# A differential-attention and mixture-of-experts kernel: set-up moved, statistics derived, and another order within a round

## The chip, the core and the metric

The kernel runs on one core of a Trainium2 chip. The core's engines work side by side, each on its own in-order queue: TensorE (PE, with its weight loads shown apart as PEld), VectorE (DVE), ScalarE (ACT), GpSimd (POOL) and SyncE (SP), which here only issues DMAs. They meet through semaphores. TensorE writes PSUM; VectorE and ScalarE read it[...]. The metric is the device time of one launch in microseconds; the time of a kernel is the median of its runs.

## The reference

Input x has 8 sequences of 512 tokens and 128 features, all in fp32. The first half is differential attention with 16 heads of 8 features, the second a mixture of 8 experts (hidden width 512) of which each token takes 2. Each half ends in a residual and a layer norm.

```python
s1, s2 = q @ k1.T * SCALE, q @ k2.T * SCALE          # per head, causal mask
attn = softmax(s1) - sigmoid(lambda)[head] * softmax(s2)
attn = attn / max(sum(abs(attn)), 1e-6)
x = layernorm(x + (attn @ v) @ Wo.T)                 # no scale, no shift

xn = (x - mean(x)) * rsqrt(var(x) + 1e-5) * gamma + beta
w, idx = top_k(softmax(xn @ router_w.T / 1.5), 2)
y = sum over the two experts of w * (silu(xn @ W1[e]) @ W2[e])
x = layernorm(x + y)
```

So two norms follow each other: the layer norm at the end of attention, and, on its result, the norm that feeds the router and the experts. With S1 and S2 the sums of the unnormalised exponentials E1 and E2, attn is proportional to E1 - c E2 with c = sigmoid(lambda) S1/S2, and the sum of absolute values is worked out from the sum over max(E1, c E2).

## The kernel before

**Units and slots.** Attention is tiled in units of 32 queries (Q) times 4 heads on the 128 partitions, four head groups beside each other. A sequence has 16 units (j = 0 to 15); unit j looks at L = 32 (j + 1) keys. A unit with L up to 256 has two slots, each of two head groups and both score sets; a wider one has four slots, of two groups and one set. That makes 48 slots in a sequence and 384 in all, the "score slots" of the prediction. Four units make a block of 128 tokens, and 32 blocks the input.

**A round.** `round_of(now, ahead)` (L1122) writes out by hand, for all engines, what is issued for one slot. Its order sets the order of every engine's queue:

1. TensorE: the product with V (`times_v`, tile po) for a unit whose transposed weights are complete, and after a block's last unit its first block task; then the scores of the slot ahead (`scores`, L366 and the mask L375).
2. ScalarE: the copies of transposed weights out of PSUM (`evacuate`, aT, L512), then the queue `on_act`.
3. VectorE: the negated row maxima of this slot (`maxima`, tile nm, L388 for narrow and L396 for wide units).
4. TensorE: the transposes of what was combined a round ago (`transposes`, tile pt, L487). The two weight sets are added up in PSUM by transposing both into one tile.
5. VectorE: the queue `on_dve`, which holds whatever tasks of the round before have put there.
6. VectorE and GpSimd: `combine` (L424). Ahead of a unit's first piece `ratios` forms c1 = S1 sigmoid(lambda) and c2 = c1/S2 (L418 to L422). Then VectorE computes max(c2 E2, E1) into junk and its sum (L432), and GpSimd multiplies E2 by -c2 in place (L442). It must not start before VectorE has read E2.
7. ScalarE: the exponentials of this slot with their sums (`exps`, L406); then the queue `on_dve_late` on VectorE, which finishes the silu of the experts (hT, L881).
8. One task from `misc` (blocks, projections of the next sequence), and one from `routing` if there is any; one indirect transfer on GpSimd, from `moves` (sending rows to their experts, L811) or `gathers` (fetching results, L959); and expert tasks from `experts` as far as a pace allows. At most two of these allocate PSUM tiles pm, which have two buffers.

**Blocks.** A finished block runs through `block_tasks` (L537), one task to a round: reciprocals (rd, rexp), `normalise`, `project_out` with the residual xa and its statistics, `first_norm` (x1 and its own statistics), `second_norm` (xh), `turn` (transpose to xnT), `logits`. Reciprocal square roots are a power on GpSimd (`rstd_of`, tile l_rs, L112).

**Chunks.** Blocks are routed in chunks of 6, 9, 9 and 6 blocks, with the rows sent to their experts' tiles of 128, and a last chunk of 2 that computes all experts. `route_tasks` (L639) is a list of steps of small VectorE operations; `together` joins two of them in one round (weights with chosen, starts with rows). An expert tile is `turn` (pa, xgT, ysb) and `hidden` (pz, th, hT).

**Set-up.** Ahead of the rounds come constants (memsets on GpSimd), loads, the rearranged weights wq_sb and wk_sb, sigmoid of lambda (slam, L225) and slam + 1 (L226), the copies i4 and mk for the mask (L218, L219), wo_sb (L228), the zero fill of the experts' row buffers in DRAM (L271), and the projections of the first sequence: xT (L292), q (qs, then four scaled heads qb on GpSimd, L301), k, v (vt, with eight rearranging DMAs into vr, L327).

Of the kernel before, what the change touches and what calls it, by code (L numbers as in the profile page):

```python
# [20 lines left out]
def kernel(  # L21
# [15 lines left out]
    nc = tc.nc  # L37
# [28 lines left out]
    nc.gpsimd.memset(nhalf, -0.5)  # L66
    rank = const.tile([P, CB, E], F32, name="rank")
    for e in range(E):
        nc.gpsimd.memset(rank[:, :, e : e + 1], float(E - e))
# [6 lines left out]
    nc.gpsimd.memset(before, 1.0)  # L76
    nc.gpsimd.affine_select(
        out=before,
        in_=before,
        pattern=[[1, P]],  # L80
        compare_op=ALU.is_ge,
        fill=0.0,
        base=-1,
        channel_multiplier=-1,
    )
    ones = const.tile([P, P], BF16, name="ones")
    nc.gpsimd.memset(ones, 1.0)

    upto = const.tile([P, E, E], F32, name="upto")
    for e in range(E):  # L90
        nc.gpsimd.memset(upto[:, e, : e + 1], 1.0)
        if e + 1 < E:
            nc.gpsimd.memset(upto[:, e, e + 1 :], 0.0)

    fill = const.tile([P, E, CB], F32, name="fill")
    for k in range(CB):
        nc.gpsimd.memset(fill[:, :, k : k + 1], float(P * k))
# [6 lines left out]
    for t in range(tiles_of(CB)):  # L104
        nc.gpsimd.memset(number[:, t, :], float(t))
# [28 lines left out]
    with ExitStack() as actx:  # L134
# [52 lines left out]
        for h in range(4):  # L187
            nc.scalar.dma_start(
                slam[Q * h : Q * h + Q, :],
                lam.rearrange("(g h) -> h g", h=4)[h].partition_broadcast(Q),  # L190
            )
# [5 lines left out]
        nc.scalar.dma_start(gam, gamma.unsqueeze(1))  # L197
        nc.scalar.dma_start(bet, beta.unsqueeze(1))
        nc.scalar.dma_start(rw_sb, rw)
# [14 lines left out]
        nc.vector.tensor_reduce(hm, hsel, AX.X, ALU.max)  # L214
        nc.vector.tensor_scalar_mul(hms, hm, SCALE)
        for g in range(NG):
            r = slice(32 * g, 32 * g + 32)
            nc.vector.tensor_copy(i4[r], identb[r, r].unsqueeze(1).to_broadcast([32, 4, Q]))  # L218
            nc.vector.tensor_copy(mk[r], maskb[r, r])  # L219
# [5 lines left out]
        nc.scalar.activation(slam, slam, AF.Sigmoid)  # L225
        nc.vector.tensor_scalar(slam1, slam, 1.0, None, ALU.add)  # L226
        for h in range(4):
            nc.vector.tensor_scalar_mul(wo_sb[:, h, :], won, hm[:, h : h + 1])  # L228

# [31 lines left out]
        nc.gpsimd.memset(zero, 0.0)  # L261
# [6 lines left out]

        for c in chunks:
            if c.sparse:  # L270
                nc.sync.dma_start(  # L271
                    c.xs.rearrange("(t p) d -> p t d", p=P),
                    zero.unsqueeze(1).to_broadcast([P, c.nt, D]),
                )
        chunk_of = {n: c for c in chunks for n in range(c.n0, c.n0 + c.nb)}

        def projection_tasks(b):
# [16 lines left out]
            def project_q():  # L294
                pm = ps_m.tile([P, T], F32, tag="pm", name=f"pmq_{b}")
                nc.tensor.matmul(pm, lhsT=wq_sb, rhs=xTf, start=True, stop=True)

                def spread():
                    nc.vector.tensor_copy(qs, pm)
                    for h in range(4):  # L300
                        nc.gpsimd.tensor_scalar(  # L301
                            qb[:, :, h, :],
                            qs.rearrange("p (j q) -> p j q", q=Q),
                            hms[:, h : h + 1],
                            1.0,
                            ALU.mult,
                            ALU.mult,
                        )
# [24 lines left out]
        class Unit:  # L333
# [80 lines left out]
            def ratios(self):  # L414

                sums, jj = self.blk["sums"], self.jj
                c1 = sp.tile([P, NG], F32, tag="c1", name=f"c1_{self.b}_{self.j}")
                nc.vector.tensor_mul(c1, sums[:, 0, jj, :], slam)  # L418
# [3 lines left out]
                nc.vector.tensor_mul(self.c2, c1, r2)  # L422

            def combine(self, piece):  # L424
# [5 lines left out]
                L = self.L  # L430
                for g in piece:
                    nc.vector.scalar_tensor_tensor(  # L432
                        junk[:, :L],
                        self.et[:, g, 1, :L],
                        self.c2[:, g : g + 1],
                        self.et[:, g, 0, :L],
                        ALU.mult,
                        ALU.max,
                        accum_out=self.blk["big"][:, self.jj, g : g + 1],
                    )  # L440
                for g in piece:
# [7 lines left out]
                    )  # L449
                for gs, lo, kw in self.blocks(piece):  # L450
# [86 lines left out]
        def block_tasks(b, i, blk):  # L537
# [39 lines left out]
            def project_out():  # L577
# [10 lines left out]
                def residual():  # L588
# [4 lines left out]
                    s["xa"], s["mv"], s["rs"] = xa, mv, rstd_of(bp, mv, 1, "l1")  # L593
# [3 lines left out]
            def first_norm():  # L597
                def norm():
                    x1 = s["x1"] = ch.x1[:, ci, :]
                    nc.vector.tensor_scalar(  # L600
                        x1, s["xa"], s["mv"][:, 0, 0:1], s["rs"], ALU.subtract, ALU.mult
                    )
                    mv = bp.tile([P, 1, 2], F32, tag="mv2", name=f"mv2_{n}")
                    stats_of(bp, x1, mv[:, 0, :], "l2")
                    s["mv2"], s["rs2"] = mv, rstd_of(bp, mv, 1, "l2")

                on_dve.append(norm)

            def second_norm():
                def norm():  # L610
                    if ch.sparse:
                        s["xh"] = ch.xh[:, ci, :]
                    else:
                        s["xh"] = bp.tile([P, D], F32, tag="xh", name=f"xh_{n}")
                    nc.vector.tensor_scalar(
                        s["xh"], s["x1"], s["mv2"][:, 0, 0:1], s["rs2"], ALU.subtract, ALU.mult
                    )

                on_dve.append(norm)

# [645 lines left out]
```

## Time and profile before

| | |
|---|---|
| median of 3 runs | 1222.89 us (1214.82 to 1224.34) |
| the profiled execution, its own time | 1229.11 us |
| its span | 1227.1 us |
| mean granted TensorE clock | 0.923 |
| first row maxima (L388) | 20.54 us |
| last row maxima of attention (L396) | 1105.57 us |
| indirect transfers issued on GpSimd, rows sent and rows fetched | 65.4 and 60.9 us, 60 each |

The profile belongs to one execution. "Busy" is the share of the span in which an engine has an instruction under way; TensorE's matmuls are pipelined and their ends modelled, so its busy share overstates how near it is to its peak. PEclk gives the TensorE clock that was granted, in tenths of full speed, in 40 equal slices. A line of the timeline has the start, the time, the engine, the source line, the operation, the tile written and the tile read, how many instructions are merged, and in brackets the idle time of that engine just before and what ended it. In the list of waits the engine named first stood idle until the one behind the arrow was done. Idle time of an engine that nobody waits for costs nothing.

### The profile page before, as it was taken

How to read it: one execution, taken by the hardware profiler on the slowest of the kernel's cores; microseconds unless marked ns; L12 is line 12 of the kernel's file. 1: busy time of each engine (PE TensorE's matmuls, PEld its weight loads, DVE VectorE, ACT ScalarE, POOL GpSimd, SP SyncE). 2: the span in 40 equal slices, each digit the busy share in tenths (PEclk: the TensorE clock that was granted, in tenths of full speed). 3: DMA queues.
4: the chain of work that ended last, by engine and by line, in shares of the span. 5: the costliest groups of instructions: out<-in, count | busy, mean ns of one | idle time of the engine just before them, and what ended most of it. 6: DMA issues, size and time to landing. Idle time of an engine off the chain costs nothing.

```text
span 1227.1 us, 28291 instructions
## 1 busy us (share of the span) xinstructions
PE 1101.6 (90%) x9450; PEld 779.6 (64%) x9450; DVE 948.4 (77%) x2900; ACT 782.7 (64%) x2776; POOL 543.0 (44%) x967
## 2 busy tenths in 40 slices
PE   4999899888999899989898899988899889997786
PEld 2556555555666666666566666665667667776675
DVE  4688778867888678887689888879767897975656
ACT  4578767557777667766576777776567665763221
POOL 4343434464433343356556442343643762364333
PEclk8699969878999789997899999999989998999998
DMA  8000000011121111110133113221222333435762
GB/s 245 7 8 1 10 2 8 26 59 30 30 82 45 33 42 53 46 41 23 38 99 85 57 45 91 63 56 47 72 78 72 105 107 105 126 92 149 215 188 68
DMA packets 128897, 84.30 MB, mean 69 GB/s; under 512 B 22896, under 2 KB 114288, under 8 KB 128752
## 3 DMA queue, kind: packets, MB, share of 16 engines
q1 hardware_dynamic: 110944, 68.25, 19.8%
q0 software_dynamic: 3840, 7.87, 2.3%
q10 hardware_dynamic: 13968, 6.37, 1.8%
q8 instruction: 76, 1.25, 0.4%
q14 instruction: 69, 0.57, 0.1%
HBM read 63.31 MB, written 17.56 MB: 66 GB/s over the span
## 4 chain that ended last, share of the span: by engine, by line
PE 56%; DVE 19%; ACT 10%; issue 6%; POOL 4%; DMA 4%; ACTq 0%; SPq 0%; POOLq 0%; DVEq 0%
PE pt L487 18%; PE sc L366 12%; ACT et L406 6%; PE po L529 5%; PE sc_None L366 5%; PE pa L914 5%; PE pz L934 4%; DVE junk L432 3%; DVE nm L396 3%; DVE nm L388 2%; PE pmo L580 2%; ACT aT L512 2%; DVE l_st L118 1%; DMA got<-ys,row 1%; POOL qb L301 1%
## 5 line engine op out<-in xcount | busy, mean ns | idle before, releaser
L442 POOL TENSOR_SCALAR et<-et,c 128x224 f32<-128x224 f32 (+15 forms) x512 | 266.9, 526 | 438.6 <-DVE junk L432 301.2
L487 PE MATMUL pt<-ident,et 128*128 128x128 f32 (+1 forms) x2048 | 330.0, 297 | 36.6 <-POOL et L442 20.7
L406 ACT ACTIVATE et<-sc,nm 128x512 f32<-128x512 f32 (+7 forms) x512 | 299.7, 593 | 68.8 <-DVE nm L396 46.8
L487 PEld LDWEIGHTS pt<-ident,et 128*128 128x128 f32 (+1 forms) x2048 | 231.9, 146 | 171.6 <-issue 59.9
L396 DVE TENSOR_REDUCE nm<-sc 128x2 f32<-128x576 f32 (+7 forms) x256 | 251.6, 983 | 41.8 <-PE sc L375 41.5
L432 DVE SCALAR_TENSOR_TENSOR junk<-et,c 128x224 f32<-128x224 f32 (+15 forms) x512 | 264.2, 516 | 9.6
L512 ACT COPY aT<-pt 128x384 f32<-128x384 f32 (+5 forms) x488 | 185.8, 407 | 130.5 <-PE pt L487 127.4
L366 PE MATMUL sc<-kT,qb 32*128 32x384 f32 (+7 forms) x1024 | 246.5, 558 | 13.3 <-ACT et L406 12.4
L406 ACT ACTIVATE et<-sc_None,nm 128x256 f32<-128x256 f32 (+7 forms) x512 | 188.1, 385 | 31.2 <-DVE nm L388 23.2
L366 PE MATMUL sc_None<-kT,qb 32*128 32x512 f32 (+7 forms) x512 | 118.6, 546 | 22.3 <-ACT et L406 21.1
L388 DVE TENSOR_REDUCE nm<-sc_None 128x4 f32<-128x256 f32 (+7 forms) x128 | 96.0, 751 | 40.8 <-PE sc_None L375 40.5
L366 PEld LDWEIGHTS sc<-kT,qb 32*128 32x128 f32 x1024 | 78.4, 187 | 63.7 <-ACT et L406 30.6
L112 POOL TENSOR_TENSOR l_rs<-l_ve,nhalf 128x1 f32<-128x1 f32 x96 | 62.5, 651 | 124.9 <-DVE l_ve L110 102.8
L934 PE MATMUL pz<-xgT,w 128*128 128x128 f32 x704 | 101.5, 291 | 11.4 <-DVE xgT L908 10.7
L406 ACT ACTIVATION_READ_ACCUMULATOR et<-sc_None,nm 128x1 f32 x512 | 107.4, 210 | 0.0
L406 ACT ACTIVATION_READ_ACCUMULATOR et<-sc,nm 128x1 f32 x512 | 103.2, 202 | 0.0
L934 PEld LDWEIGHTS pz<-xgT,w 128*128 128x128 f32 x704 | 92.0, 203 | 16.7 <-DVE xgT L908 13.5
L914 PE MATMUL pa<-w,hT 128*128 128x128 f32 x704 | 100.0, 289 | 0.6 <-ACT ysb L924 0.6
L914 PEld LDWEIGHTS pa<-w,hT 128*128 128x128 f32 x704 | 93.2, 206 | 1.9 <-issue 1.2
L879 ACT ACTIVATE th<-pz 128x512 f32<-128x512 f32 x88 | 52.7, 599 | 58.3 <-PE pz L934 52.1
L529 PE MATMUL po<-aT,vt 128*32 128x128 f32 (+1 forms) x2048 | 85.2, 291 | 0.0
L811 POOL DMA_INDIRECT xs<-xh,row x60 | 65.4, 1089 | 42.9 <-DMA xs<-xh,row 30.8
(148 smaller groups left out, 1316.2 us busy)
## 6 DMA issues: line engine op xcount, KB each, us to landing
w<-in_w_dram SPq DMA_DIRECT2D x192, 256.0 KB, 3.0
xg<-xs SPq DMA_DIRECT2D x88, 64.0 KB, 3.3
ys<-ysb ACTq DMA_DIRECT2D x88, 64.0 KB, 1.5
xs<-zero SPq DMA_DIRECT2D x2, 1600.0 KB, 13.8
xs<-zero SPq DMA_DIRECT2D x2, 1216.0 KB
xt<-in_x_dram SPq DMA_DIRECT2D x8, 256.0 KB
out_dram<-ot SPq DMA_DIRECT2D x32, 64.0 KB, 2.1
vr<-vt SPq DMA_DIRECT2D x32, 32.0 KB, 1.9
```

The costliest lines, as they stand in the source:

```text
L366: nc.tensor.matmul(parts[gi][:, :, :L], lhsT=qb[r, j].rearrange("p h q -> p (h q)"), rhs=kT[r, sets, :L], start=True, stop=False,)
L388: nc.vector.tensor_reduce(self.nm[:, g, :], sc.rearrange("p g (s l) -> p g s l", s=2)[:, :, :, : self.L], AX.X, ALU.max, negate=True,)
L396: nc.vector.tensor_reduce(self.nm[:, g, s], sc[:, :, : self.L], AX.X, ALU.max, negate=True)
L406: nc.scalar.activation(self.et[:, g, si, : self.L], sc[:, gi, lo : lo + self.L], AF.Exp, bias=self.nm[:, g, si : si + 1], accum_out=self.b ...
L432: nc.vector.scalar_tensor_tensor(junk[:, :L], self.et[:, g, 1, :L], self.c2[:, g : g + 1], self.et[:, g, 0, :L], ALU.mult, ALU.max, accum_ ...
L442: nc.gpsimd.tensor_scalar(self.et[:, g, 1, :L], self.et[:, g, 1, :L], self.c2[:, g : g + 1], -1.0, ALU.mult, ALU.mult,)
L487: nc.tensor.matmul(pt[: len(gs) * kw, x_, :], lhsT=lhsT, rhs=ident, is_transpose=True, start=(k == 0), stop=(k == 1),)
L512: nc.scalar.copy(self.aT[: rows[done], self.used + done : self.used + end, :], pt[: rows[done], done:end, :],)
L529: nc.tensor.matmul(self.blk["po"][32 * g : 32 * g + 32, self.jj, :], lhsT=v[:rows, kb, 32 * g : 32 * g + 32], rhs=self.aT[:rows, self.at[g ...
L811: nc.gpsimd.indirect_dma_start(ch.xs[:, :], bass.IndirectOffsetOnAxis(ap=ch.row[:, k, c : c + 1], axis=0), ch.xh[:, c, :], None,)
L914: nc.tensor.matmul(pm[:, 1, :], lhsT=hT[y][:, f, :], rhs=w[y][1][:, f, :], start=(f == 0), stop=(f == NF - 1),)
L934: nc.tensor.matmul(pz[:, f, :], lhsT=w[t][0][:, f * P : (f + 1) * P], rhs=xgT[t], start=True, stop=True,)
```

## The change

**Set-up.** Constants that the first rounds don't need are set behind the first projections. The first projections now stand in the region whose order is written by hand: x is transposed and copied first, then hm and hms, q, k and v, then i4 and mk, slam, slam1 and wo_sb, the constants, and last the zero fill. Loads of lambda, gamma, beta and the router's weights are issued by SyncE in place of ScalarE. The sigmoid is computed as (tanh(lambda/2) + 1)/2.

**Statistics.** The second norm's reciprocal deviation is derived from the first variance v, as (v (1 + eps) + eps^2)^-0.5, in the same power operation of two columns; x1 and xh are both formed from xa.

**Order.** `combine` comes right behind `maxima`, and `on_dve` behind it. For L up to 96 the maximum is taken after GpSimd's scaling, for a whole piece in one operation with a reduction behind it, on `on_dve_late`.

**Routing.** One step to a round, and only in rounds in which `misc` is empty; `together` is gone.

**GpSimd.** c1 is computed there (`weighted`), at the end of a unit's last round. The four qb heads of a projection go one to a round (`on_pool`), ahead of moves and gathers. The tiles w1st, w2nd and row come from a pool of three buffers in place of two.

```diff
-            nc.scalar.dma_start(
+            nc.sync.dma_start(
                 slam[Q * h : Q * h + Q, :],
...
-        nc.scalar.activation(slam, slam, AF.Sigmoid)
...
+                    on_pool.extend(lambda h=h: spread_head(h) for h in range(4))
...
-                nc.vector.tensor_mul(c1, sums[:, 0, jj, :], slam)
...
-                nc.vector.tensor_mul(self.c2, c1, r2)
+                nc.vector.tensor_mul(self.c2, self.c1, r2)
+
+            def weighted(self):
+                self.c1 = sp.tile([P, NG], F32, tag="c1", name=f"c1_{self.b}_{self.j}")
+                nc.gpsimd.tensor_tensor(self.c1, self.blk["sums"][:, 0, self.jj, :], slam, ALU.mult)
...
+                L, g0, m = self.L, piece[0], len(piece)
+                small = L <= 96
+                def largest():
+                    first, second = (self.et[:, g0 : g0 + m, k, :L] for k in range(2))
+                    big = self.blk["big"][:, self.jj]
+                    if small:
+                        both = junk[:, : m * L].rearrange("p (g l) -> p g l", g=m)
+                        nc.vector.scalar_tensor_tensor(both, second, -1.0, first, ALU.mult, ALU.max)
+                        nc.vector.tensor_reduce(big[:, g0 : g0 + m], both, AX.X, ALU.add)
+                        return
...
+                if not small:
+                    largest()
                 for g in piece:
                     nc.gpsimd.tensor_scalar(
                         self.et[:, g, 1, :L],
...
+                if small:
+                    on_dve_late.append(largest)
...
-                    s["xa"], s["mv"], s["rs"] = xa, mv, rstd_of(bp, mv, 1, "l1")
+                    ve = bp.tile([P, 2], F32, tag="l1_ve", name=f"l1_ve_{n}")
+                    nc.vector.tensor_scalar(ve[:, 0:1], mv[:, 0, 1:2], EPS, None, ALU.add)
+                    nc.vector.tensor_scalar(
+                        ve[:, 1:2], mv[:, 0, 1:2], 1.0 + EPS, EPS * EPS, ALU.mult, ALU.add
+                    )
+                    rs = bp.tile([P, 2], F32, tag="l1_rs", name=f"l1_rs_{n}")
+                    nc.gpsimd.tensor_tensor(rs, ve, nhalf[:, :2], ALU.pow)
...
-                    stats_of(bp, x1, mv[:, 0, :], "l2")
-                    s["mv2"], s["rs2"] = mv, rstd_of(bp, mv, 1, "l2")
...
-                        ch.w = [r["rc"], cp.tile([P, CB], F32, tag="w2nd", name=f"w2nd_{n0}")[:, :nb]]
+                        ch.w = [r["rc"], x1p.tile([P, CB], F32, tag="w2nd", name=f"w2nd_{n0}")[:, :nb]]
...
-            tasks = [largest, first, second, together(weights, chosen), counts]
-            tasks += [together(starts, rows), owners]
+            tasks = [largest, first, second, weights, chosen, counts]
+            tasks += [starts, rows, owners]
...
-            run(on_dve)
             left = now["left"] if now else 2
             for _ in range(-(-len(to_combine) // left)):
                 v, piece = to_combine.popleft()
                 v.combine(piece)
                 to_transpose.append((v, piece))
+            run(on_dve)
...
-            if routing:
+            elif routing:
...
             for _ in range(1 if now else 2):
-                if moves:
+                if on_pool:
+                    on_pool.popleft()()
+                elif moves:
                     moves.popleft()()
...
+            if now and now["left"] == 1:
+                now["u"].weighted()
...
+            nc.scalar.activation(slam, slam, AF.Tanh, scale=0.5)
+            nc.vector.tensor_scalar(slam, slam, 1.0, 0.5, ALU.add, ALU.mult)
```

## The prediction

> **What bounds the kernel now.** I read the busy shares first, then the waits, then single rounds in order of time, and last the granted clock of short windows.
>
> ```profile
> PE 1101.6 (90%) x9450; PEld 779.6 (64%) x9450; DVE 948.4 (77%) x2900; ACT 782.7 (64%) x2776; POOL 543.0 (44%) x967
> PEclk8699969878999789997899999999989998999998
> ```
>
> TensorE is busy nine tenths of the span, so no edit can win more than its 125 us of idle time, unless the clock rises too: it is below full in about half of the slices. The waits, longest first, say what the idle time waits for:
>
> ```profile
> POOL et L442 <- DVE junk L432: 301.2, 180, 8.0
> ...
> DVE xgT L908 <- ACT ysb L924: 50.7, 51, 4.6
> ...
> PE sc_None L366 <- ACT et L406: 21.1, 31, 1.6
> PE pt L487 <- POOL et L442: 20.7, 24, 3.5
> ```
>
> (Columns: total us, times, longest.) The chain is VectorE's junk (the maximum of the two weight sets, L432), then GpSimd's scaling of et in place (L442), then TensorE's transpose pt (L487). GpSimd idles 301 us behind junk; only 20.7 us of that reach TensorE. The 21.1 us in rows of short width belong to ScalarE's exponentials, which no edit shortens. One round of the second kind, in order of time:
>
> ```profile
> 848.71 0.23 DVE L758 TENSOR_TENSOR r_more<-r_cnt,fill 128x72 f32<-128x72 f32 x1
> ...
> 851.36 0.17 DVE L786 CAST row<-r_pos 128x18 uint32<-128x18 f32 x1
> ...
> 851.92 0.48 DVE L432 SCALAR_TENSOR_TENSOR junk<-et,c 128x256 f32<-128x256 f32 x1
> ...
> 852.61 1.13 POOL L442 TENSOR_SCALAR et<-et,c 128x256 f32<-128x256 f32 x2 [3.99 <-DVE junk L432]
> ...
> 853.33 1.51 PE L487 MATMUL pt<-ident,et 128*128 128x128 f32 x7 [2.34 <-POOL et L442]
> ```
>
> Two routing steps run together stand ahead of junk for 2.8 us, and TensorE stops for 2.34. The other pattern is GpSimd itself blocked by the four qb heads in one piece:
>
> ```profile
> 593.72 2.90 POOL L301 TENSOR_SCALAR qb<-qs,hms 128x512 f32<-128x512 f32 x4
> ...
> 597.15 0.55 PE L487 MATMUL pt<-ident,et 128*128 128x128 f32 x3 [3.53 <-POOL et L442]
> ```
>
> What such a stop costs beyond itself stands in windows of time (length, then busy time of PE, PEld, DVE, ACT, POOL, the granted clock, DMA):
>
> ```profile
> 873.00:885.00 12.00, 12.00 (x111) 8.73 (x109) 9.98 (x27) 7.85 (x26) 7.76 (x12) 1.00 0.32 87
> 885.00:903.00 18.00, 16.35 (x96) 11.71 (x95) 9.45 (x24) 7.91 (x27) 9.29 (x13) 0.62 0.19 59
> ```
>
> After two stops of 0.98 and 0.67 us (at 886.06 and 888.51) the clock is 0.62 for 18 us: TensorE is full and slow, 18 x 0.38 = 6.8 us lost. I walked the span in windows of 3 us and summed length x (1 - clock): 96 us. About 51 follow the short rows at starts of batches, some 15 stand in and near the tail, 29 follow waits for POOL et.
>
> **The change, part by part** (sums against the profiled execution, 1229.1 us, 2.0 more than its span; the median 1222.9 is 6.2 less).
>
> *Set-up.*
>
> ```profile
> 11.79 0.20 ACT L225 ACTIVATE slam<-slam 128x4 f32<-128x4 f32 x1
> ...
> 13.63 0.69 DVE L292 COPY xT<-pmx 128x512 f32<-128x512 f32 x1
> 14.37 0.50 PEld L296 LDWEIGHTS pmq<-xT,wq_sb 128*128 128x128 f32 x2 [8.00 <-DVE xT L292]
> ...
> 20.54 0.49 DVE L388 TENSOR_REDUCE nm<-sc_None 128x4 f32<-128x128 f32 x2
> ```
>
> xT (VectorE, in order) waits behind slam1, which waits for the sigmoid, its table and its DMA. Afterwards xT follows the weight copies, which end at 7.6, so the projections come 6.0 us earlier and vt ends at 14.4 in place of 20.4. But the i4 and mk copies (1.49 us), two slam operations (0.34) and wo_sb (0.88) now stand behind vt: 14.4 + 2.7 = 17.1 for the first maximum, against 20.54. Gain 3.4, not 6. The table load of 1.28 us becomes one load in place of two. On SyncE seven small loads come ahead of vr (2.8 us by their ScalarE rows: 4 x 0.39, 0.44, 0.46, 0.34), free by then; vr's eight issues of 0.62 us pass in front of the zero fill that held SyncE 14.75 us, so po's wait for vr (2.13 us at 31.63) goes too. The fill then lies between vr and the second x, from about 20 to 35 us; x is used near 60, the filled rows first near 244: no cost. The constants' memsets, 2.9 us of GpSimd, go behind the first qb and end before the first coefficient is due. Sum -5.5, between -3 and -8.
>
> *Order on VectorE, single routing steps, qb heads one to a round.* Of TensorE's stops of 0.3 us and more on POOL et I take those whose cause is edited: at 227.44, 845.10, 853.33 (routing ahead of junk: 1.16, 0.68, 2.34), at 75.85, 193.60, 326.05, 597.15, 867.60 (qb heads: 1.20, 1.19, 0.30, 3.53, 0.99), at 886.06 and 888.51 (normalisation ahead of junk). Sum 13.0. The rest (261.48, 265.41, 648 to 653 and others, near 7) stand behind indirect sends and stay. So -13; between -5 and -17, since TensorE may meet a later wait, for aT.
>
> *The clock behind those stops.* Windows 228-240 (5.1), 597-606 (3.4), 852-873 (3.4), 885-903 (6.8): 18.7 us. Here a rule bears. The Trainium skill's page "TensorE: Matmul & The Clock Gate", part 1 ("The HAM clock gate"), says the ramp penalty is under 1% of a typical kernel's span and need not be fitted; by it all 96 us would be at most 12, and this term 18.7 x 12/96 = 2.3. The granted clock of these rows says 96, so the row decides. Whether a stretch disappears with its stop is open: the short-row stops of 0.9 us do the same. I take three quarters, -14, between 0 and -19.
>
> *Second statistics derived.* For each of 32 blocks a bn_stats (295 ns) and a bn_aggr (182) go: 15.3 us of VectorE; one power of 651 ns on GpSimd goes, 20.8 us; one round of latency. It is taken as zero on TensorE's path, since VectorE has 23% idle; with the next parts -2, between 0 and -10.
>
> *c1 to GpSimd.* 128 products leave VectorE (173 ns mean, 22.1 us). Nearest row: the two-input power on GpSimd, 128x1, 547 ns at least, 651 mean. The page "GPSIMD Engine Reference", § Engine selection, speaks against it: elementwise work belongs on VectorE, GpSimd being about 2x slower for two inputs. By rule or by row, 128 x (0.65 - 0.17) = +61 us if it all lay on the path. It doesn't: c1 starts at the last exponential, while VectorE is still in the next maximum (0.75 to 1.22 us from L396); in the round at 764.74 exponentials end at 765.28 and the maximum at 765.74. Exposed is 0.2 us in perhaps a third of units, on VectorE. What queues behind the waiting c1 is the next scaling, which needs it anyway. Where c1 stands behind an indirect send (1.09 us, plus waits of 30.8 us in all) the coefficient and junk follow late. I take +2, between -10 and +10.
>
> *Narrow rows (L up to 96).* Four junk with read become two plus two reductions, and wait for two scalings (0.58 us) ahead of the next maximum; scaling no longer waits for junk. +1, between -3 and +6.
>
> *What comes later.* Evacuations of pm (xgT, on, xT) now follow one or two junk (0.60 + 0.08 at width 384). Counting from the last reader of each pm buffer to TensorE's next write, two thirds of the buffers that VectorE frees have over 2 us to spare, and of those in the moved part some 20 less than 0.8. +3, between 0 and +8.
> Routing steps also wait for block tasks now. In the built order the third chunk's counting moves from score slot 304 to 320 of 384, its first expert tile from 334 to 346; both reach the last tile at 381, with the same tail. Six or seven tiles (1.06 + 1.06 + 0.27 us of TensorE) leave 940 to 981 us for later. Where TensorE is full that is neutral; the loss is that the last batch's short rows get bare, and bare starts fall to half clock (153 to 177: 10.2 us lost). +4, between 0 and +10. That ch.w and ch.row come from a pool of three buffers in place of two is taken as nothing: no wait on them is seen.
>
> Sum: -5.5 - 13 - 14 - 2 + 2 + 1 + 3 + 4 = -24.5: 1204.6 as profiled, 1198 at the level of the median.
>
> **Rivals.** *Nothing but set-up (0.2):* each closed stop runs into the next wait, as TensorE waits for aT in stops of 0.68 us, and the half-clock stretches arise from short rows anyway: -5.5 - 6.5 + 9 = -3, so 1220. For it: 90% busy; against: the clock is full in most rounds without such a stop.
> *More (0.17):* the 29 us of clock behind POOL et all go, and ScalarE's 70 us of waits for maxima (46.8 + 23.2) shrink by a fifth: -24.5 - 15 - 7, about 1177.
> *Slower (0.13):* xgT and the other evacuations behind junk. In attention rounds run 69 expert tiles; if each stops TensorE for one junk, 0.6 us, that is +41: 1198 + 41 = 1239. It decides from 24.5/69 = 0.36 us per tile, where nothing is left of the gain. Against it: TensorE's waits for xgT (10.7 us) lie nearly all in the tail, and xgT itself has waited for ScalarE's ysb 50.7 us with junk queued behind it; that queue is now the other way round.
> *The likeliest (0.5):* 1184 to 1212.
>
> **How the numbers follow.** Forecast 1198. The range 1168 to 1234 takes in the first two rivals and part of the third. A measurement here tells about 1% (12 us): faster is below 1210.7, slower above 1235.1. Faster: nearly all of the likeliest and all of "more", 0.66; same: "set-up only" and edges, 0.22; slower 0.12.
>
> **What would show it.** First maximum near 17 us and no wait of po for vr; no routing operation between a maximum and junk; PE waits on POOL et below 9 us; clock full near the routing of each chunk; c1 near 0.6 us on GpSimd. I am wrong if TensorE's waits for xgT grow by over 20 us, if VectorE idles long for c1, or if the clock's loss stays at 96.

## The result: the changed kernel is 0.6% slower

| | before | after |
|---|---|---|
| median of 20 runs each | 1224.12 us (1214.82 to 1239.67) | 1231.38 us (1222.80 to 1247.25) |
| ratio | | 1.006, 95% interval 1.0038 to 1.0083 |
| the profiled execution, its own time | 1229.11 us | 1227.28 us |
| its span, granted clock | 1227.1 us, 0.923 | 1225.6 us, 0.930 |

The forecast was 1198 us, a gain. The medians in this document are over all executions, while the ratios, their intervals and the means of the clock leave out those more than 1.5% above the fastest of their kernel, which trims a few kernels hard (both_back keeps 10 of 22, c1_back and c1_ahead 4 of 6, c1_order_back 2 of 8), so the table of experiments gives the quotient of the medians beside each ratio.

The two profiled executions stand the other way round than the medians. What follows from a trace here is therefore where something happens; what it is worth comes from runs.

The page of the changed kernel, busy times and the granted clock in 40 slices:

```profile
PE 1095.5 (89%) x9450; PEld 774.0 (63%) x9450; DVE 922.6 (75%) x2613; ACT 780.5 (64%) x2775; POOL 554.1 (45%) x1063
PEclk7699989889999899889778999999998998998998
```

VectorE has lost 287 instructions and 26 us of work, and the end has not come earlier: its busy time was not the bound. TensorE's clock has holes in other places, the largest behind the start in slices 20 to 22.

Some of its waits between 22 and 1104 us (total us, times, longest):

```profile
DVE c L381 <- POOL c L385: 38.2, 27, 3.8
...
PE pt L466 <- POOL et L419: 8.2, 7, 2.4
PE pml L618 <- DVE xnT L613: 5.6, 9, 1.5
PE pmn L607 <- DVE xh L594: 5.1, 6, 2.3
```

The wait that the prediction aimed at went as forecast: TensorE stood 20.7 us for POOL et before and 8.2 us now (forecast: below 9). New is the first line: VectorE stands 38.2 us, 27 times, for c1 from GpSimd. The same stretch of time as a whole, before and after (length, then busy time of PE, PEld, DVE, ACT, POOL, granted clock, DMA share, GB/s):

```profile
22.00:1104.00 1082.00, 1003.16 (x8748) 693.80 (x8752) 872.47 (x2669) 745.06 (x2697) 489.20 (x829) 0.92 0.20 56
```

```profile
22.00:1104.00 1082.00, 998.36 (x8780) 690.32 (x8778) 847.05 (x2386) 746.84 (x2700) 500.47 (x926) 0.93 0.21 59
```

TensorE is idle for 83.6 us of it, against 78.8 before: the stops for et went and others came, for aT (11.3 to 14.1), xh (0.9 to 5.1), xnT (none to 5.6) and xgT (0.5 to 4.7).

One stop in order of time shows a late c1 on the way to TensorE:

```profile
227.95 1.06 POOL L795 DMA_INDIRECT xs<-xh,row  x1 [0.44 <-DMA xs<-xh,row]
229.04 0.21 POOL L385 TENSOR_TENSOR c<-sums,slam 128x4 f32<-128x4 f32 x1
229.28 0.16 DVE L381 TENSOR_TENSOR c<-c,r 128x4 f32<-128x4 f32 x1 [2.18 <-POOL c L385]
229.48 0.69 DVE L406 SCALAR_TENSOR_TENSOR junk<-et,c 128x448 f32<-128x448 f32 x1
...
232.76 1.30 DVE L594 TENSOR_SCALAR xh<-xa,mv,l_rs 128x128 f32<-128x128 f32 x1
...
234.12 0.33 PE L607 MATMUL pmn<-ident,xh 128*128 128x128 f32 x1 [2.31 <-DVE xh L594]
```

c1 (POOL c) takes 0.21 us, but it is issued behind an indirect send of 1.06 us that had itself waited 0.44 us for the send before. VectorE stands 2.18 us at c2, and what stands behind c2 in its queue comes later: junk, the residual, the statistics, then xh. (How much of the 2.18 us reaches xh was not measured: xh is issued a round later, behind other work, and itself takes 1.30 us here against a median of 0.36 for its group.) TensorE stops for 2.31 us. And then the clock goes to half (columns as above):

```profile
234.00:252.00 18.00, 17.88 (x107) 10.86 (x111) 9.96 (x21) 7.79 (x23) 9.51 (x13) 0.53 0.06 19
...
852.00:903.00 51.00, 48.17 (x424) 33.62 (x420) 41.97 (x118) 33.97 (x108) 17.73 (x33) 1.00 0.17 48
597.00:633.00 36.00, 34.67 (x195) 20.02 (x192) 19.26 (x44) 16.60 (x54) 13.03 (x20) 0.53 0.21 61
```

A stop of 2.31 us is followed by 18 us at 0.53, which is 8.5 us lost. Near 597 us, where the prediction counted 3.4 us to be won, 36 us run at 0.53 and 17 are lost; the stop ahead of that stretch is one of 0.56 us for et, at 595.63, and no c1 stands in it. The stretches around 852 to 873 and 885 to 903 us, which cost 10.2 us before, are at full clock as hoped. So of the four windows that were to be won, two went and two grew.

**Two shares of a span.** Every execution has a span and a mean granted clock, so each span can be split into what the clock lost, span x (1 - clock), and the rest, span x clock. Over 19 runs of after and 97 of before (the latter from the three groups of runs below) the means are:

| | clock | lost to the clock | the rest |
|---|---|---|---|
| before | 0.9317 | 83.6 us | 1139.7 us |
| after | 0.9246 | 92.7 us | 1136.7 us |
| difference (2 standard errors) | | +9.1 (2.8) | -3.0 (1.5) |

The rest is 3 us shorter, and the clock takes 9 us more. The split overstates the clock somewhat, since a part of a slow stretch hides in waits that would have come anyway: over the runs of before on three chips the span falls by 8.0, 8.2 and 6.7 us for each 0.01 of clock (fitted lines through 32, 44 and 30 runs), where the split counts 1224 x 0.01 = 12.2. Taking two thirds, the clock's 9.1 is worth 6 us of the 7.3 by which the medians differ.

The profile that the prediction was built on, with a clock of 0.923 and some 96 us lost, was an execution with less clock than most: the mean of before is 0.9317 and 83.6 us.

### The profile page after: what moved, and what is told of

It reads as the page before. It is cut to its first block, busy times and chain, and to the rows that moved or that the text cites. A ratio compares the mean times of both kernels' runs of the same rounds, so it can differ in the third digit from the quotient of the medians.

```text
span 1225.6 us, 27961 instructions
## 1 busy us (share of the span) xinstructions
PE 1095.5 (89%) x9450; PEld 774.0 (63%) x9450; DVE 922.6 (75%) x2613; ACT 780.5 (64%) x2775; POOL 554.1 (45%) x1063
## 4 chain that ended last, share of the span: by engine, by line
PE 53%; DVE 21%; ACT 8%; issue 8%; POOL 5%; DMA 4%; ACTq 0%; POOLq 0%; DVEq 0%; SPq 0%
PE pt L466 16%; PE sc L327 13%; PE po L508 6%; ACT et L367 5%; DVE junk L406 4%; PE pz L911 4%; PE pa L891 4%; PE sc_None L327 3%; DVE nm L357 3%; DVE nm L349 3%; DMA xs<-xh,row 2%; ACT aT L491 2%; POOL got L936 1%; PE pmo L559 1%; POOL et L419 1%
## 5 line engine op out<-in xcount | busy, mean ns | idle before, releaser
L419 POOL TENSOR_SCALAR et<-et,c 128x224 f32<-128x224 f32 (+15 forms) x512 | 274.8, 543 | 419.1 <-DVE junk L406 320.0
L466 PE MATMUL pt<-ident,et 128*128 128x128 f32 (+1 forms) x2048 | 325.3, 297 | 28.4 <-ACT aT L491 16.2
L327 PE MATMUL sc<-kT,qb 32*128 32x384 f32 (+7 forms) x1024 | 252.6, 570 | 12.6 <-ACT et L367 11.6
L406 DVE SCALAR_TENSOR_TENSOR junk<-et,c 128x128 f32<-128x128 f32 (+12 forms) x416 | 230.8, 555 | 7.1
L327 PE MATMUL sc_None<-kT,qb 32*128 32x512 f32 (+7 forms) x512 | 108.6, 503 | 25.0 <-ACT et L367 23.6
L349 DVE TENSOR_REDUCE nm<-sc_None 128x4 f32<-128x256 f32 (+7 forms) x128 | 95.5, 747 | 18.6 <-PE sc_None L336 18.3
L858 DVE SCALAR_TENSOR_TENSOR hT<-th,pz 128x512 f32<-128x512 f32 x88 | 60.2, 684 | 41.7 <-ACT th L856 40.5
```

The lines of the kernel that those rows point to most:

```text
L327: nc.tensor.matmul(parts[gi][:, :, :L], lhsT=qb[r, j].rearrange("p h q -> p (h q)"), rhs=kT[r, sets, :L], start=True, stop=False,)
L349: nc.vector.tensor_reduce(self.nm[:, g, :], sc.rearrange("p g (s l) -> p g s l", s=2)[:, :, :, : self.L], AX.X, ALU.max, negate=True,)
L406: nc.vector.scalar_tensor_tensor(junk[:, :L], second[:, k], self.c2[:, g : g + 1], first[:, k], ALU.mult, ALU.max, accum_out=big[:, g : g ...
L419: nc.gpsimd.tensor_scalar(self.et[:, g, 1, :L], self.et[:, g, 1, :L], self.c2[:, g : g + 1], -1.0, ALU.mult, ALU.mult,)
L466: nc.tensor.matmul(pt[: len(gs) * kw, x_, :], lhsT=lhsT, rhs=ident, is_transpose=True, start=(k == 0), stop=(k == 1),)
```

## Experiments

All kernels compute the whole of the reference. "Lost" and "rest" are differences of the two shares from the runs of before in the same group, with two standard errors in brackets.

| kernel | ratio to before, 95% interval | quotient of the medians | lost to the clock | the rest |
|---|---|---|---|---|
| after | 1.0060 [1.0038, 1.0083] | 1.0059 | +9.1 (2.8) | -3.0 (1.5) |
| c1_back | 0.9870 [0.9820, 0.9920] | 0.9913 | +4.0 (9.4) | -16.4 (4.3) |
| order_back | 1.0146 [1.0101, 1.0191] | 1.0136 | +34.8 (8.0) | -15.6 (3.3) |
| routing_back | 0.9941 [0.9913, 0.9969] | 0.9930 | -8.1 (4.3) | +1.6 (2.3) |
| setup_only | 0.9926 [0.9890, 0.9961] | 0.9917 | -1.4 (5.5) | -4.8 (2.3) |
| both_back | 0.9838 [0.9803, 0.9873] | 0.9896 | -11.1 (6.2) | -8.5 (2.8) |
| c1_ahead | 0.9864 [0.9803, 0.9926] | 0.9923 | -2.5 (12.0) | -12.1 (4.3) |
| routing_beside | 0.9930 [0.9897, 0.9963] | 0.9947 | -6.0 (4.5) | -3.2 (2.3) |
| c1_only | 1.0084 [1.0049, 1.0119] | 1.0064 | +8.9 (4.0) | +1.4 (3.1) |
| c1_order_back | 0.9959 [0.9872, 1.0046] | 1.0063 | +14.2 (28.4) | -18.5 (10.4) |
| c1_ahead_beside | 0.9873 [0.9823, 0.9922] | 0.9872 | -10.5 (4.8) | -5.4 (3.0) |
| stats_only | 0.9919 [0.9884, 0.9954] | 0.9903 | -11.2 (3.6) | -0.5 (3.2) |
| qb_only | 0.9986 [0.9961, 1.0011] | 0.9999 | +6.7 (5.1) | -8.6 (2.7) |

### One part undone, and the set-up alone

**c1_back.** The changed kernel with c1 on VectorE again, in `ratios`:

```diff
+                self.weighted()
                 self.c2 = sp.tile([P, NG], F32, tag="c2", name=f"c2_{self.b}_{self.j}")
...
-                nc.gpsimd.tensor_tensor(self.c1, self.blk["sums"][:, 0, self.jj, :], slam, ALU.mult)
+                nc.vector.tensor_mul(self.c1, self.blk["sums"][:, 0, self.jj, :], slam)
...
-            if now and now["left"] == 1:
-                now["u"].weighted()
```

> The changed kernel with the product c1 back on VectorE, right ahead of the reciprocal. Theory 'c1 behind sends' (VectorE waited 38.2 us for c1 on GpSimd, up to 3.8 us at a time, behind indirect sends, and everything on VectorE with it): faster than the changed kernel by 10 us or more, near 1220 where the changed one has 1231. Theory 'steps behind junk' and theory 'third chunk late': within 4 us of the changed kernel.

Measured: median 1218.02 against 1228.66 us, ratio 0.987. Against after (1.006) that is 0.987/1.006 = 0.981: c1 on GpSimd costs this kernel 1.9%, some 23 us (1.4% or 18 us by the medians), where the prediction put +2 and bounded it at +10. Most of it is rest, which is 13.4 us shorter than in after (-16.4 against -3.0), so it is not the clock alone.

**order_back.** The changed kernel with `on_dve` ahead of `combine` again:

```diff
                 to_evacuate.append((v, piece, v.transposes(piece)))
+            run(on_dve)
             left = now["left"] if now else 2
...
                 to_transpose.append((v, piece))
-            run(on_dve)
```

> The changed kernel with the queue of VectorE steps run ahead of combining again. Theory 'steps behind junk' (TensorE's new stops on xh, xnT, on and xgT, 16 us before the tail, with the half clock behind them): faster than the changed kernel by 10 us or more, and these stops back below 3 us, with some of the stops on POOL et back. Theory 'c1 behind sends' and 'third chunk late': no gain, or a loss of up to 5 us since junk stands behind the steps again.

Measured: median 1245.41 us, ratio 1.0146. The new order gains 1.006/1.0146 = 0.9915, so 0.85%. The theory that the evacuations behind junk are what costs is refuted as the cause of the loss. Its mechanism is there all the same: without the new order the rest is 12.6 us shorter (-15.6 against -3.0), and the clock loses 25.7 us more (+34.8 against +9.1). The order buys clock and pays part of it in later evacuations. The waits of order_back show the first half of that:

```profile
DVE c L381 <- POOL c L385: 40.2, 30, 4.2
...
PE pt L466 <- POOL et L419: 14.4, 17, 2.7
```

TensorE stands for et 17 times in place of 7, while VectorE's wait for c1 stays as it was. TensorE's stops for xnT are gone, but those for xh stay (5.6 us), which the theory expected to be closed by this.

**routing_back.** The changed kernel with routing beside `misc` and joined steps, as before:

```diff
-            elif routing:
+            if routing:
...
-            tasks = [largest, first, second, weights, chosen, counts]
-            tasks += [starts, rows, owners]
+            tasks = [largest, first, second, together(weights, chosen), counts]
+            tasks += [together(starts, rows), owners]
```

> The changed kernel with routing steps joined and run beside block tasks as before, all else changed. Theory 'third chunk late' (score slots 352 to 383 took 114.4 us against 99.3 before): 352 to 383 back near 100 us and the whole faster by 6 to 10 us. The other two theories: within 4 us, since what the last stretch loses was won in the slots before it (352 was reached 20 us earlier than before).

Measured: median 1220.03 us, ratio 0.9941, against after 0.988. The routing part costs after 1.2%, and all of it is clock: lost -8.1 against +9.1, the rest +1.6 against -3.0. In its profile the slots 352 to 383 take 101.4 us, near the 100 that the theory 'third chunk late' expected; the lines stand under routing_beside.

**setup_only.** The kernel before with the block of the new set-up alone (the loads on SyncE, projections first, the constants and the zero fill behind them, tanh for the sigmoid).

> The kernel before with the new set-up alone. By the trace of the changed kernel (first row maxima at 18.87 us against 20.54, and no wait of po for vr): 3 to 5 us faster than before, near 1220. If starts are swallowed by the half clock of the first 30 us: no difference.

Measured: median 1218.45 us, ratio 0.9926, or 9 us; by the means of the split it is 6, of which 4.8 are rest and next to nothing clock, close to the -5.5 of the prediction. TensorE's wait of po for vr is gone in the trace of setup_only, as forecast. In the trace of after the first maxima come at 18.87 us, not at 17.1:

```profile
8.20 2.08 PE L255 MATMUL pmq<-xT,wq_sb 128*128 128x512 f32 x2 [1.36 <-DVE xT L251]
...
14.40 0.69 DVE L284 COPY vt<-pmv 128x512 f32<-128x512 f32 x1 [3.40 <-PE pmv L281]
...
15.01 1.73 DVE L1178 COPY i<-identb 32x128 bf16<-32x128 bf16 x1
15.11 1.65 DVE L1179 COPY mk<-maskb 32x32 bf16<-32x32 bf16 x1
15.60 0.93 POOL L1206 MEMSET number<- 128x8 f32 x25
16.81 0.50 PE L336 MATMUL sc_None<-mk,i 32*128 32x64 bf16 x2 [2.08 <-DVE mk L1179]
18.87 0.48 DVE L349 TENSOR_REDUCE nm<-sc_None 128x4 f32<-128x128 f32 x2
```

The projections start at 8.20 us, 6.2 earlier than before (the prediction had 6.0). vt ends at 15.09 us, 0.7 later than reckoned. Then the first pair of i4 and mk copies, overlapping, lasts until 16.8 us, beside GpSimd's memsets, and TensorE waits 2.08 us for the mask. The prediction had put all eight copies at 1.49 us from the trace of before, where GpSimd was not at work beside them. The memsets end at 16.69 us, and the three pairs behind them take 0.16 to 0.19 us for each copy, so that the memsets hold the first pair up fits; it was not tried by itself.

### What is it in c1 and in the routing

**both_back.** c1_back and routing_back together.

> The changed kernel with c1 back on VectorE and the routing steps joined and run beside block tasks, as before; set-up, derived statistics, combining behind the maxima and single qb heads stay. If the two costs are separate they add up: -1.9% for c1 and -1.2% for routing against the changed kernel (1.006 of before) make 0.975 of before, near 1198. If they are one loss seen twice: not below 0.985.

Measured: median 1214.58 against 1227.36 us, ratio 0.9838, the lowest of the ratios; by the medians, 0.9896, it is not. The product of the two would be 0.987 x 0.9941/1.006 = 0.975, outside the interval (0.979 by the medians): the two parts share some of their cost.

**c1_ahead.** c1 stays on GpSimd, and is issued ahead of the round's heads, sends and fetches, not behind them:

```diff
+            if now and now["left"] == 1:
+                now["u"].weighted()
             for _ in range(1 if now else 2):
                 if on_pool:
                     on_pool.popleft()()
...
-            if now and now["left"] == 1:
-                now["u"].weighted()
```

> The changed kernel with c1 on GpSimd, but issued ahead of the round's qb head or indirect transfer instead of behind it. Theory 'behind sends' (c1 itself takes 0.20 us; what costs is the queue ahead of it): most of the gain of taking c1 back to VectorE, 0.99 of before, and VectorE's waits for c1 below 10 us in place of 38. Theory 'the hop itself costs' (any c1 on GpSimd holds VectorE, or the waiting c1 holds the sends behind it): no better than 1.00 of before.

Measured: median 1217.87 us, ratio 0.9864, as good as c1 on VectorE (0.987). Two lines moved up win 0.9864/1.006 = 0.981 (0.986 by the medians), and the rest is 9.1 us shorter than in after. Its waits between 22 and 1104 us:

```profile
DVE c L381 <- POOL c L385: 19.6, 15, 3.2
...
PE pt L466 <- POOL et L419: 5.0, 7, 1.2
PE pml L618 <- DVE xnT L613: 3.5, 8, 1.1
PE pmn L607 <- DVE xh L594: 2.6, 4, 1.4
```

VectorE's wait for c1 is halved, not below 10 us as expected, and TensorE's stops for et, xnT and xh fall from 18.9 to 11.1 us together. As far as these intervals tell, it is not GpSimd's multiplication that costs but its place in the queue. In the window behind the stop shown above, this kernel runs at nearly full clock, but not in that of the other long stretch:

```profile
234.00:252.00 18.00, 16.27 (x161) 10.71 (x162) 13.13 (x28) 12.85 (x42) 12.77 (x17) 0.95 0.08 23
...
597.00:633.00 36.00, 35.90 (x234) 22.71 (x233) 23.56 (x55) 19.23 (x54) 13.80 (x22) 0.65 0.27 80
```

In the same 18 us TensorE completes 161 matmuls in place of 107. That a late c1 makes such stretches is not shown by this. c1_back, in which nothing waits for GpSimd's c1, has one of 27 us in nearly the same place, behind a stop of 1.08 us for ScalarE's exponentials:

```profile
214.50:241.50 27.00, 27.00 (x148) 16.46 (x145) 18.73 (x55) 12.63 (x37) 8.62 (x12) 0.50 0.09 27
```

And order_back, in which VectorE waits for c1 as long as in after, runs from 225 to 252 us at full clock.

**routing_beside.** The changed kernel with `elif routing` made `if routing`, the steps still single.

> The changed kernel with routing steps still single, but run beside block tasks. If the cost of the new routing is that it stands aside for block tasks and so brings the third chunk late: as good as routing wholly back, 0.994 of before or below, since the single steps leave VectorE's pieces short. If it is the splitting that costs: near 1.006, like the changed kernel.

Measured: median 1220.91 us, ratio 0.993, like routing_back (0.9941). So it is the standing aside for `misc` that costs, not the splitting of the steps. Where it costs is not settled. The stretch from slot 352 to slot 383, with the third chunk's tiles in it, in after, in routing_beside and in routing_back:

```profile
986.50:1101.00 114.50, 107.58 (x970) 84.57 (x970) 94.49 (x267) 69.47 (x207) 58.69 (x84) 0.97 0.45 126
```

```profile
983.80:1082.70 98.90, 95.45 (x894) 73.30 (x895) 82.82 (x228) 66.58 (x203) 42.02 (x67) 1.00 0.41 115
```

```profile
991.90:1093.30 101.40, 97.27 (x902) 74.45 (x903) 81.94 (x224) 65.42 (x198) 41.37 (x66) 1.00 0.42 122
```

After takes 15.6 us longer for it than routing_beside, but does 76 matmuls more, 12.1 us of TensorE: most of it is deferred work. Beside routing_beside, after is 7.5 us late at slot 96, 14.1 at slot 240, 2.7 at slot 352 (its third chunk not yet begun), 18.3 at slot 383 and 13.8 at the end. By this pair of executions the 14 us were lost before slot 240, where after has its half-clock stretches of 234 to 252 and 597 to 633 us, and the late third chunk returns what it had deferred. The execution of routing_back tells it otherwise: it is 7.1 us behind after at slot 96 and 5.4 at slot 352, and gains 13.1 us in the last stretch, where after does 68 matmuls more.

**c1_ahead_beside.** c1_ahead and routing_beside together.

> The changed kernel with c1 issued ahead of the round's transfer on GpSimd and routing steps single but beside block tasks: two moved statements. From 0.986 and 0.993, each against 1.006: 0.974 if they add, 0.984 if they overlap as with c1 on VectorE (0.984). Better than both kernels either way, 1194 to 1208.

Measured: median 1207.88 against 1223.5 us, ratio 0.9873, faster than both kernels. The product would be 0.9864 x 0.993/1.006 = 0.974, outside the interval. Once c1 is out of the way of the sends, letting the routing run beside `misc` gains nothing by the ratios (0.9864 and 0.9873) and half a per cent by the medians (0.9923 and 0.9872), less than its 1.2% in the changed kernel either way.

**c1_only.** The kernel before, with c1 on GpSimd at the end of a unit's last round.

> The kernel before with c1 on GpSimd at the end of a unit's last round, and nothing else. Theory 'behind sends': slower than before by 1.5 to 2%, near 1250. If c1 costs only where combining comes right behind the maxima: within 0.5% of before, since steps that run ahead of combining cover the wait.

Measured: median 1235.24 us, ratio 1.0084, less than the 1.5 to 2% expected. The rest grows by 1.4 us, within its error, and the clock loses 8.9. Its waits:

```profile
DVE c L420 <- POOL c L424: 34.8, 27, 3.0
...
PE pt L489 <- POOL et L444: 21.5, 25, 3.6
```

The wait on VectorE is nearly that of after, yet TensorE's stops hardly change: 21.5 us for et, 20.7 in before, and 1.1 for xh, 0.9 in before. In the order of before the loss is about half as large as in that of after. One reason offers itself, and was only argued: there the block tasks of a round stand ahead of c2 in VectorE's queue, and a late c1 holds up junk alone.

**c1_order_back.** Both undone, to see whether the order's gain depends on c1.

> The changed kernel with both c1 back on VectorE and the queue of steps ahead of combining. Order alone cost 0.9% to take back (1.0146 against 1.006) with c1 on GpSimd; c1 alone cost 1.9% (0.987). Theory 'the waiting c1 costs more where combining comes first, since every step on VectorE stands behind it': this kernel near 1.006 (c1 worth 0.8% here, as in the kernel before, and the new order worth 1.9% once c1 is off GpSimd). If the two are independent: near 0.995.

Measured: median 1231.15 us, ratio 0.9959 with an interval of 0.987 to 1.0046. The medians (1.0063) lie at the one expectation, near 1.006, the ratio at the other, near 0.995. It does not tell the two apart, and the question stays open.

### Two more parts alone

**stats_only.** The kernel before with the second statistics derived (`norms` in place of `first_norm` and `second_norm`).

> The kernel before with the derived second statistics alone: 15 us of VectorE and 21 us of GpSimd less, one round less for a block. Off the path, as the prediction had it: within 0.5% of before. If VectorE's relief reaches TensorE: 0.99 or below.

Measured: median 1211.65 us, ratio 0.9919, just outside the half per cent expected. The rest is unchanged (-0.5), the clock loses 11.2 us less. So this part is worth 10 us, all of it clock. Whether the step less in the block's chain or the time saved on VectorE and GpSimd does it, and which stop of TensorE it saves, was not isolated.

**qb_only.** The kernel before with the four qb heads one to a round:

```diff
-                    for h in range(4):
-                        nc.gpsimd.tensor_scalar(
+                    on_pool.extend(lambda h=h: spread_head(h) for h in range(4))
...
-                if moves:
+                if on_pool:
+                    on_pool.popleft()()
+                elif moves:
```

> The kernel before with the four qb heads one to a round alone. By the prediction's stops behind them (75.85, 193.60, 326.05, 597.15, 867.60: 7.2 us) and the half clock after two of these (5 us): 0.990 to 0.994 of before. If the sends that now wait for the heads cost as much: 1.00.

Measured: median 1223.36 against 1223.5 us, ratio 0.9986: nothing, where 0.990 to 0.994 was expected. The split tells why: the rest falls by 8.6 us, somewhat more than the 7.2 of the five stops that the prediction listed for qb heads, and the clock loses 6.7 us more. In its trace TensorE's stops for et are 11.1 us in place of 20.7: the stops went, and the slow clock came elsewhere.

## Why the prediction was wrong, point by point

| step of the prediction | it said | the runs |
|---|---|---|
| set-up | -5.5 | right in sum: rest -4.8 alone; first maxima 1.8 us later than worked out |
| order, single steps, qb heads: stops | -13 | TensorE's stops for et fell by 12.5 (20.7 to 8.2), and 17.3 us of others came |
| the clock behind those stops | -14 | **failed**: the clock loses 9.1 us more |
| derived statistics, with the next parts | -2 | -0.81% alone, 10 us, all of it clock |
| c1 to GpSimd | +2 | **failed**: 1.4 to 1.9% in the changed kernel, 18 to 23 us; 0.84% alone |
| narrow rows | +1 | not tried alone; VectorE's new wait for the scalings is 11.1 us, 14 times |
| what comes later: evacuations | +3 | order_back, without them, has 12.6 us less of rest; an estimate of some 4, if a third of the 25.7 us of clock belongs to the rest |
| what comes later: third chunk | +4 | 1.2% for standing aside, 15 us; by the third chunk or not is open |

**The step "c1 to GpSimd ... I take +2" failed first.** Its duration was overstated, and the term came out too small nonetheless. It took the two-input power (651 ns) as the nearest row; c1 takes 203, and took 173 on VectorE in the kernel before, so that the factor of two for two inputs that the prediction quoted does not show at this size either:

```profile
L385 POOL TENSOR_TENSOR c<-sums,slam 128x4 f32<-128x4 f32 x128 | 25.9, 203 | 57.9 <-ACT et L367 56.4
...
L381 DVE TENSOR_TENSOR c<-c,r 128x4 f32<-128x4 f32 x128 | 22.1, 172 | 49.4 <-POOL c L385 38.2 <-DVE r L380 1.0
```

```profile
L418 DVE TENSOR_TENSOR c<-sums,slam 128x4 f32<-128x4 f32 x128 | 22.1, 173 | 1.9 <-ACT et L406 1.9
```

The prediction saw that c1 would sometimes stand behind an indirect send and wrote "the coefficient and junk follow late"; it did not multiply that out. The order of magnitude was in reach: in the trace of before a send is 1.09 us and waits 30.8/60 = 0.5 us on average for its predecessor, 120 indirect transfers are issued by the same rounds, and c1 was put behind the transfer of its round. How often VectorE would be caught could not be read there; in after it is 27 waits of 1.4 us on average, 38 us. It also counted the waiting instruction's cost only for the coefficient, and not for what stands behind it in VectorE's queue: the residual, the statistics and xh, which TensorE waits for. c1_ahead isolates the place in the queue: the same multiplication on the same engine, ahead of the head or transfer of its round, and the cost is gone. By which stops of TensorE it costs is argued from the traces, and c1_only loses without such stops.

**The step "the clock behind those stops ... -14" failed second.** It charged the clock only to stops that go. The parts that were run alone or undone have a clock price too, in either direction, and for several it is the larger share: +8.9 against +1.4 us for c1 alone, -11.2 against -0.5 for the statistics, +6.7 against -8.6 for the qb heads, about -26 against +13 for the order. In these traces stretches of half clock with TensorE full do follow stops of half a microsecond to two, as the prediction said, but not every stop is followed by one: in after one of 1.67 us at 908.21 us is not. And which stop is followed, and for how long, did not survive the change: two of the four stretches went and two grew. 96 us, from an execution with less clock than most, were also the wrong start. The rule that was set aside, of the Trainium skill's page "TensorE: Matmul & The Clock Gate", part 1 (under 1% of the span), is said there of the ramp; taken for all lost clock, as the prediction took it, it does not hold here: the mean loss of before is 83.6 of 1223 us, 7%, and two thirds of it, by the fitted lines, show in the span. For the change, though, its -2.3 would have been nearer to the measured +9.1 than -14.

**The routing.** "+4" foresaw that work gets late and that bare rounds fall to half clock. The amount is 15 us in place of 4. The place is open: one pair of executions puts it ahead of slot 240, another into the last batch. That it shrinks or vanishes when c1 is mended would fit if both parts starve TensorE in the same rounds, those in which blocks, sends and routing of a chunk come together; that was only argued.

**The rivals.** At the level of the prediction's median the ratio makes 1230. "Nothing but set-up", 1220, and "slower", 1239, are about equally near. The first clause of the former is what happened: closed stops ran into other waits. "Slower by xgT behind junk" had the right sign and the wrong cause: TensorE's stops for xgT grew by 4 us (0.5 to 4.7), not by 41, and undoing the order makes the kernel slower. Among its own signs of error, the prediction named "if VectorE idles long for c1"; that came, and so did the last one in a stronger form, since the clock's loss did not fall but rose by 9.1 us.

**The sum of the parts.** Set-up -0.74%, statistics -0.81%, qb heads -0.14% (alone in the kernel before), order -0.85%, c1 +1.9%, routing +1.2% (undone in the changed kernel) add up to +0.6%, which is what was measured. Since c1 and routing overlap when both are undone, that agreement says less than it seems.

Open: what makes half-clock stretches choose their places, where the routing's cost arises, why the statistics alone spare 11 us of clock, and whether the order's gain needs c1's place.

## What to carry to other kernels

When a small operation moves to another engine, price the queue that it lands in and the queue of the engine that will wait for it, not its duration: 0.2 us of work behind a 1.1 us send cost 1.4 to 1.9%, and two lines moved up won it back. Where the granted clock is below full in much of the span, split the span of several runs into lost clock and the rest before forecasting, and give a clock price to added waits as well as to removed ones. Of a bundle of edits, run the parts alone: this one held about 1% of gain (0.8 to 1.6% in c1_ahead_beside, c1_ahead and both_back, by medians and ratios), hidden mostly by the place of two lines.

## What was not expected of the hardware

- A c1 multiplication of 128x4 takes 203 ns on GpSimd, less than a third of the one-column power there (a mean of 651 in the trace of before); in the trace of after the two-column power takes 710 ns (median), the one-column power 570.
- VectorE's first i4 and mk copies, beside GpSimd's memsets, last 1.73 and 1.65 us (1.95 and 1.87 in setup_only); all eight were 1.49 us together in the trace of before.
- VectorE's xh at 232.76 us (1.30 us, median 0.36) and the x1 behind it (1.11) end together near 234.1 us, just after an indirect send and a scaling on GpSimd end (232.18 to 233.98). That GpSimd holds VectorE up there fits, and was not tried by itself.
- The mean granted clock of one and the same kernel varies from run to run (before: standard deviation 0.006 over 97 runs), and the span follows it by 6.7 to 8.2 us for each 0.01.
